# A graph layer on one core: two more quads of sender rows are loaded by ScalarE, and the last groups are taken in another order

## The chip, the core and the metric

The kernel runs on one core of a Trainium2 chip. The core has five engines that run side by side, each working through its own list of instructions in order: TensorE (PE, matrix products), VectorE (DVE), ScalarE (ACT), GpSimd (POOL) and SyncE (SP, which only issues transfers). They wait for each other through semaphores, which are counters. ScalarE, GpSimd and SyncE can issue transfers between the memory of the chip and that of the core. The metric is the device time of one execution in microseconds, lower is better.

## The reference, cut to what matters

There are 6250 nodes with 128 features each and 206,250 edges, sorted by receiver. Each edge gets a weight vector of 128 from two small networks over its 32 + 32 features. It is multiplied with the receiver's query and the sender's key and summed in 8 heads of 16, which gives one score for each head. The score scales the sender's value, and the results are summed for each receiver. The sum is added to the node's features, and a layer norm follows.

```python
w_ij = silu(edge_feats @ rad_W1 + rad_b1) @ rad_W2 + rad_b2
w_ij = w_ij + (silu(chi_scalar @ sph_W1 + sph_b1) @ sph_W2 + sph_b2)
q_i = (node_feats @ Wq)[receivers]; k_j = (node_feats @ Wk)[senders]; v_j = (node_feats @ Wv)[senders]
alpha = (q_i * w_ij * k_j).reshape(-1, 8, 16).sum(axis=-1) / sqrt(16) * cutoffs[:, None]
out = segment_sum(alpha[..., None] * v_j, receivers) / 16
x = layernorm(x + out)
```

All of it is in float32.

## The kernel before

Edges are worked on in **quads** of 512 (4 columns of 128) and **groups** of four quads (2048 edges). There are 403 quads in 101 groups; the last group has three. A group's quads are taken in the order 0, 2, 1, 3, and each place in this order is a **slot**. The loop in L583 to L643 goes over groups and slots. Inside a slot the calls are written out by hand, and this order is kept on every engine (`manual_schedule`, L191), so the order of the calls is the order in each engine's list.

First comes a stage over the nodes (L207 to L364). Keys and values of all nodes are put into one table in the chip's memory (`kv_tab`, 1 KB a node). Ten quads (`XQ`) get their keys and values there directly, from gathered node features.

In the loop, a quad goes through these steps:

- Its senders' rows of `kv_tab` have been fetched into the core. `gathers` (L144) does this with four indirect transfers issued by GpSimd (L121), each of 128 rows, into a ring of 16 buffers (`RING`), 14 slots ahead (`AHEAD`).
- For six quads (`ROW_QUADS`), spread evenly, `load_rows` (L152) does it instead through SyncE: for each of the 128 edges of a column one register load of four addresses (L164) and four transfers of 1 KB (L168), a few edges in each slot, done eight slots (`ROW_LEAD`) ahead of use. These have two buffers of their own.
- `q_and_hidden` (L416), in every even slot: queries of two quads at their edges (L414), and the first layer of the two quads that follow (L407), then its activation on ScalarE (L432).
- `weigh` (L435): second layer on TensorE (L439), bias on ScalarE, which makes `w` (L441). `multiply` (L446) makes `u` on VectorE, and `turn_back` (L452) transposes `u` in the next slot.
- `scores` (L458 to L461) multiplies with the keys and sums the heads; `messages` (L471) scales the values.
- `sum_quads` (L481) sums a group's messages for 32 receivers a quad. `part_sums` (L509), `place` (L503) and `sum_group` (L514, L516) put them at their rows and carry over what belongs to the next group.
- `statistics` (L520) makes the layer norm. It collects four groups (`LB`), except at the end, and `write_rows` (L543) sends one group a slot to the chip's memory through SyncE.

For group g + 2, `load_x` is issued in slot 0 of group g, and `load_feats` (L173) and `load_rel` (L182) in slot 1; all three go through SyncE. The features of group g + 2 are first used by TensorE in slot 2 of group g + 1. Every transfer that SyncE or ScalarE issues carries one of eight completion counters. The framework hands these round in the order in which it plans the transfers, and a transfer waits until the one before it on the same counter has landed.

The last group's sums go over 128 rows at once: `wide_one_hots` (L484) makes the matrices on VectorE, `sum_wide` (L495) the products. In the code before, the loop ends with the last quad turned but not yet scored. Then come the sums of the last group but one, the wide sums of two quads (L650 to L652), `statistics(g - 1)`, and the last quad in three pieces (L656), followed by its own layer norm (L660 to L672).

Behind all this stands a general version for inputs that break the sorted layout (L682 to L789). It is not run here.

Of the kernel before, what the change touches and what calls it, by code (L numbers as in the profile page):

```python
# [13 lines left out]
F32 = mybir.dt.float32  # L14
# [6 lines left out]
PSUM = bass.MemoryType.PSUM  # L21
DRAM = bass.MemoryType.DRAM
SP = mybir.EngineType.SP

P = 128
N = 6250
# [18 lines left out]
LB = 4  # L45
XQ = 10
RING = 16
ROW_QUADS = 6
ROW_LEAD = 8
CHECK = 20  # L50
NEIGHBORS = 16.0
# [5 lines left out]
def gnn_kernel(ctx, tc, x, src, dst, weight, edges, rad_W1, rad_b1, rad_W2, rad_b2,  # L57
# [24 lines left out]
    dst_i = const.tile([P, NT], I32, name="dst_i")  # L82
    src_i = const.tile([P, NT], I32, name="src_i")
    src_x = const.tile([P, math.ceil(XQ / NQ) * GT], I32, name="src_x")
    at_i = const.tile([P, ROW_QUADS * QT], I32, name="at_i")
    scale = const.tile([P, NT], F32, name="scale")
    w1 = const.tile([P, D], F32, name="w1")
    w2 = const.tile([P, 2, D], F32, name="w2")
# [16 lines left out]
    ends = const.tile([P, 8], F32, name="ends")  # L105
    general = const.tile([1, 1], I32, name="general")

    gp = ctx.enter_context(tc.tile_pool(name="group", bufs=2))
    ep = ctx.enter_context(tc.tile_pool(name="edge", bufs=2))


    aux = ctx.enter_context(tc.tile_pool(name="aux", bufs=1, space=PSUM))
# [4 lines left out]
    def quad_of(name, bufs, width=D):  # L117
        return ep.tile([P, QT, width], F32, name=name, bufs=bufs)
# [16 lines left out]
        else:  # L135
            pairs[-1].append(q)

    every = (len(order) - ROW_LEAD) // ROW_QUADS
    row_at = [(n + 1) * every for n in range(ROW_QUADS)]
    row_quads = {order[i] for i in row_at}  # L140
    feats_of, relb_of, act_of, kv_of, hot_of, hotT_of, x_of, q_of, msg_of = ({} for _ in range(9))
    po_of, part_of, to_of, tot_of, xT_of, y0_of, u_of, pick_of, pq_of = ({} for _ in range(9))

# [7 lines left out]

    def load_rows(i):  # L152

        k = max(i + ROW_LEAD - 1, 0) // every
        if k >= ROW_QUADS:
            return
        q, start = order[row_at[k]], max(k * every - ROW_LEAD + 1, 0)
        slots = row_at[k] - ROW_LEAD + 1 - start
        a, b = ((j * P + slots - 1) // slots for j in (i - start, i - start + 1))
        if i == start:  # L160
            kv_of[q] = quad_of("rows", 2, 2 * D)
        table = kv_tab.bitcast(U8).rearrange("(o n) b -> o (n b)", o=1)
        for p in range(a, min(b, P)):
            _, rows = nc.values_load_multi_w_load_instructions(  # L164
                at_i[p:p + 1, k * QT:(k + 1) * QT], engines=(SP,), min_val=0,
                max_val=(N - 1) * ROW_BYTES, skip_runtime_bounds_check_because="senders are nodes")
            for t in range(QT):
                nc.sync.dma_start(kv_of[q][p:p + 1, t, :].bitcast(U8),  # L168
                                  table[:, ds(rows[t], ROW_BYTES)])

    def load_feats(g):
        feats_of[g] = gp.tile([P, EG // 2], F32, name="feats")
# [34 lines left out]
    with tc.tile_pool(name="nodes", bufs=1) as nodes, \  # L207
# [145 lines left out]
                nc.sync.dma_start(scale, weight)  # L353
        for q in order[XQ:AHEAD]:
            gathers(q)
        for k, i in enumerate(row_at):
# [10 lines left out]
    with tc.tile_pool(name="ps", bufs=1, space=PSUM) as pp:  # L367
# [131 lines left out]
        def place(g):  # L499

            to = to_of[g] = gp.tile([P, 2, P], F32, name="to")
            if g < NG - 1:
                nc.vector.tensor_scalar(to[:, 0, :], colp, rowq[:, g:g + 1], None, op0=OP.is_equal)  # L503
            nc.vector.tensor_scalar(to[:, 1, :], colp, rowp[:, g:g + 1], None, op0=OP.is_equal)  # L504
# [13 lines left out]
            nc.scalar.activation(tot_of[g], ph[:, :D], AF.Copy)  # L518

        def statistics(g):  # L520
            first = g // LB * LB if g < NG - 2 else g
            if g == first:
                y0_of[g] = (gp.tile([P, LB, D], F32, name="y0"), gp.tile([P, LB, 2], F32, name="mv"))
            y0, mv = y0_of[first]
            k = g - first + 1
            nc.vector.tensor_tensor(y0[:, k - 1, :], tot_of[g], x_of[g], op=OP.add)
            st = gp.tile([P, 6], F32, name="st")
            nc.vector.bn_stats(st, y0[:, k - 1, :])
            nc.vector.bn_aggr(mv[:, k - 1, :], st)
            if k == LB or g >= NG - 3:  # L530
                sd = gp.tile([P, LB], F32, name="sd")
                nc.scalar.activation(sd[:, :k], mv[:, :k, 1], AF.Sqrt, bias=eps)
                rs = gp.tile([P, LB], F32, name="rs")
                nc.vector.reciprocal(rs[:, :k], sd[:, :k])
                shift = gp.tile([P, LB], F32, name="shift")
                nc.vector.scalar_tensor_tensor(shift[:, :k], mv[:, :k, 0], -1.0, rs[:, :k],
                                               op0=OP.mult, op1=OP.mult)
                for i in range(k):
# [44 lines left out]
        for g in range(NG):  # L583
            last = g == NG - 1
            for slot, j in enumerate((0, 2, 1, 3)):
# [22 lines left out]
                if 1 <= g:  # L608
                    for t in ((), (0, 1), (2, 3))[slot] if last else ((), (0, 1), (2,), (3,))[slot]:
                        sum_quads(g - 1, t)  # L610
                if before is not None:
                    alpha = scores(before, pu)
                multiply(q, w)
# [8 lines left out]
                if slot == 1:  # L622
                    if g + 2 < NG:
                        load_feats(g + 2)
                        load_rel(g + 2)
                    if 1 <= g:
                        place(g - 1)
                    if last:
                        place(g)
                        n = nc.values_load(general, min_val=0, max_val=1)  # L630
                if last:
                    wide_one_hots(q)
                write_rows()
                load_rows(i)
                if slot == 2 and g + 1 < NG:
                    one_hots_T(g + 1)
                if slot == 2 and 2 <= g:
                    statistics(g - 2)
                if slot == 3:
                    if g + 1 < NG - 1:  # L640
                        one_hots(g + 1)
                    if CHECK <= g < CHECK + len(checks):
                        checks[g - CHECK]()  # L643
        g = NG - 1
        pu = turn_back(before)
        part_sums(g - 1)
        sum_group(g - 1)
        po_of[g] = pp.tile([P, D], F32, name="po")
        done = [q for q in order[-quads_in(g):] if q != before]
        for q in done:  # L650
            for t in range(QT):
                sum_wide(q, t, start=(q == done[0] and t == 0))  # L652
        nc.tensor.matmul(po_of[g], to_of[g][:, 1, :], tot_of[g - 1], start=False, stop=False)
        statistics(g - 1)
        write_rows(LB)
        for t in (slice(0, 2), slice(2, 3), slice(3, 4)):  # L656
            messages(before, scores(before, pu, t), t)
            for i in range(t.start, t.stop):
                sum_wide(before, i, stop=(i == QT - 1))
        y = gp.tile([P, LB, D], F32, name="y0")[:, 0, :]  # L660
        nc.vector.tensor_tensor(y, po_of[g], x_of[g], op=OP.add)
        st = gp.tile([P, 6], F32, name="st")
        nc.vector.bn_stats(st, y)
        mv = gp.tile([P, LB, 2], F32, name="mv")[:, 0, :]
        nc.vector.bn_aggr(mv, st)
        sd = gp.tile([P, LB], F32, name="sd")
        nc.scalar.activation(sd[:, :1], mv[:, 1:2], AF.Sqrt, bias=eps)
        rs = gp.tile([P, LB], F32, name="rs")
        nc.vector.reciprocal(rs[:, :1], sd[:, :1])
        nc.vector.tensor_scalar(y, y, mv[:, 0:1], rs[:, :1], op0=OP.subtract, op1=OP.mult)  # L670

        nc.sync.dma_start(out[N - P:, :], y)  # L672

    manual.close()


    before = const.tile([P, P], F32, name="before")
    nc.vector.tensor_scalar(before, col, row, None, op0=OP.is_lt)
    spare = const.tile([P, 1], F32, name="spare")
    nc.vector.tensor_scalar(spare, row, float(NB * P), None, op0=OP.add)  # L680
# [100 lines left out]
    with tc.If(n == 0, preferred_fallthrough_block=False) as held:  # L781
        pass
    with held.Else():
        nc.sync.dma_start(acc[:N, :], x)
# [47 lines left out]
```

## Time and profile before

| | |
|---|---|
| time, median of 3 runs | 2098.6 us (2095.31 to 2099.16) |
| profiled execution, its own time | 2934.18 us |
| its span, first to last instruction | 2932.0 us |
| mean granted TensorE clock in it | 0.807 |
| GpSimd gathers from `kv_tab` | 1548, 945 ns each |
| rows of `kv_tab` loaded through SyncE | 768 register loads, 3072 transfers |
| ScalarE busy | 986.0 us (34%) |
| VectorE busy | 1458.2 us (50%) |

The profiled execution is 835.6 us longer than the median of the timed runs, so the shares of its span are not those of a timed run. Durations of single instructions, and the spacing of instructions in stretches where nothing stalls, can be read from it. In a row of the order of time, the first number is the start in us from the span's start, the second the length in us, then engine, line, operation and tiles; in brackets stand the idle time before it and what ended it. In a row of the waits stand who waited and for whom, then us in total, how many times, and the longest. In a tile row the three numbers behind the count are the shortest, median and longest duration in ns.

### The profile page before, as it was taken

How to read it: one execution, taken by the hardware profiler on the slowest of the kernel's cores; microseconds unless marked ns; L12 is line 12 of the kernel's file. 1: busy time of each engine (PE TensorE's matmuls, PEld its weight loads, DVE VectorE, ACT ScalarE, POOL GpSimd, SP SyncE). 2: the span in 40 equal slices, each digit the busy share in tenths (PEclk: the TensorE clock that was granted, in tenths of full speed). 3: DMA queues.
4: the chain of work that ended last, by engine and by line, in shares of the span. 5: the costliest groups of instructions: out<-in, count | busy, mean ns of one | idle time of the engine just before them, and what ended most of it. 6: DMA issues, size and time to landing. Idle time of an engine off the chain costs nothing.

```text
span 2932.0 us, 37165 instructions
## 1 busy us (share of the span) xinstructions
PE 2134.5 (73%) x9966; PEld 1018.8 (35%) x9966; DVE 1458.2 (50%) x3001; ACT 986.0 (34%) x1825; POOL 1502.0 (51%) x1596
## 2 busy tenths in 40 slices
PE   4776777777777777777777777676767777777777
PEld 3433333333333333333333333333333333333334
DVE  2444544545545544545455454454445545545457
ACT  1232333333332333333333333333333333323334
POOL 5355555545555545555554555545555555555540
PEclk6777878878778878888787887878778878888888
DMA  4433333333333333333333333333333333333330
GB/s 159 131 98 102 106 105 111 109 94 109 99 109 111 100 99 106 103 111 106 98 109 91 109 107 102 113 89 104 107 97 115 98 104 107 101 106 105 102 92 19
DMA packets 146344, 303.61 MB, mean 104 GB/s; under 512 B 36710, under 2 KB 79568, under 8 KB 146128
## 3 DMA queue, kind: packets, MB, share of 16 engines
q0 software_dynamic: 75584, 205.62, 24.0%
q1 hardware_dynamic: 69056, 95.15, 10.3%
q8 instruction: 81, 1.33, 0.2%
q14 instruction: 135, 1.11, 0.1%
q10 hardware_dynamic: 1488, 0.40, 0.1%
HBM read 287.58 MB, written 13.46 MB: 103 GB/s over the span
## 4 chain that ended last, share of the span: by engine, by line
PE 33%; another core or an unknown queue 16%; DVE 11%; issue 9%; ACT 5%; POOL 4%; DMA 1%; SPq 0%; DVEq 0%; ACTq 0%; POOLq 0%
PE ph L439 14%; PE pq L414 7%; PE pq L452 5%; PE ph L407 5%; POOL kv L121 4%; DVE m L458 3%; ACT w L441 3%; DVE u L446 3%; DVE msg L471 2%; ACT act L432 1%; PE po L481 1%; DVE side L460 1%; DMA kv<-kv_tab,src_i 1%; DVE to L504 0%
## 5 line engine op out<-in xcount | busy, mean ns | idle before, releaser
L121 POOL DMA_INDIRECT kv<-kv_tab,src_i x1548 | 1463.1, 945 | 1327.6 <-DVE msg L471 787.0
L439 PE MATMUL ph<-act,w 128*128 128x512 f32 x1612 | 954.0, 724 | 11.0 <-issue 9.2
L441 ACT ACTIVATE w<-ph,bsum 128x512 f32<-128x512 f32 x403 | 276.7, 687 | 1303.4 <-remote 467.6
L407 PE MATMUL ph<-feats,w 32*128 32x512 f32 x1612 | 631.0, 756 | 25.7 <-ACT w L441 23.4
L414 PE MATMUL pq<-hotT,q 32*128 32x512 f32 x806 | 385.2, 746 | 322.5 <-DVE m L458 312.9
L458 DVE TENSOR_TENSOR m<-pq,kv 128x512 f32<-128x512 f32 x399 | 274.0, 687 | 689.6 <-remote 520.7
L452 PE MATMUL pq<-ident,u 128*128 128x128 f32 x1612 | 311.8, 325 | 365.9 <-DVE u L446 267.6
L432 ACT ACTIVATE act<-ph,b 128x512 f32<-128x512 f32 x806 | 502.5, 686 | 216.3 <-PE ph L407 186.1
L446 DVE TENSOR_TENSOR u<-pq,w 128x512 f32<-128x512 f32 x403 | 277.5, 689 | 577.0 <-ACT w L441 303.0
L439 PEld LDWEIGHTS ph<-act,w 128*128 128x128 f32 x1612 | 342.1, 235 | 282.4 <-issue 277.0
L452 PEld LDWEIGHTS pq<-ident,u 128*128 128x128 f32 x1612 | 202.7, 162 | 532.9 <-issue 318.3
L414 PEld LDWEIGHTS pq<-hotT,q 32*128 32x128 f32 x806 | 101.7, 216 | 567.7 <-DVE m L458 371.3
L460 DVE TENSOR_REDUCE side<-m 128x32 f32<-128x512 f32 x405 | 280.4, 692 | 13.8
L471 DVE TENSOR_TENSOR msg<-kv,side 128x512 f32<-128x512 f32 x399 | 269.0, 674 | 0.1
L407 PEld LDWEIGHTS ph<-feats,w 32*128 32x128 f32 x1612 | 212.5, 223 | 161.1 <-issue 72.8
L481 PE MATMUL po<-msg,hot 128*32 128x128 f32 x3200 | 169.9, 313 | 0.0
L481 PEld LDWEIGHTS po<-msg,hot 128*32 128x32 f32 x3200 | 74.2, 117 | 154.0 <-issue 134.1
L518 ACT ACTIVATE tot<-ph 128x128 f32<-128x128 f32 x100 | 27.5, 275 | 197.6 <-PE ph L407 112.9
L249 PE MATMUL pk<-wkv,xT 128*128 128x256 f32 x178 | 52.3, 438 | 53.0 <-DVE kv L250 50.0
L461 DVE TENSOR_TENSOR side<-side,scale 128x32 f32<-128x32 f32 x405 | 80.7, 199 | 13.8
L387 PEld LDWEIGHTS ph<-wq,xT 128*128 128x128 f32 (+1 forms) x202 | 47.5, 236 | 70.3 <-issue 67.1
L250 DVE COPY kv<-pk 128x512 f32<-128x512 f32 (+1 forms) x45 | 30.1, 682 | 83.8 <-remote 56.1
(101 smaller groups left out, 966.9 us busy)
## 6 DMA issues: line engine op xcount, KB each, us to landing
feats<-in_edges SPq DMA_DIRECT2D x101, 512.0 KB
rows<-kv_tab SPq DMA_DIRECT2D x3072, 1.0 KB
kv<-kv_tab,src_i POOLq DMA_INDIRECT x1548
relb<-rel_lin SPq DMA_DIRECT2D x101, 128.0 KB
x<-in_x SPq DMA_DIRECT2D x101, 64.0 KB
out<-y SPq DMA_DIRECT2D x101, 64.0 KB
kv_tab<-kv SPq DMA_DIRECT2D x12, 512.0 KB
act<-in_x SPq DMA_DIRECT2D x12, 256.0 KB
```

Source lines behind the costliest of these rows:

```text
L121: nc.gpsimd.indirect_dma_start(out=o, out_offset=None, in_=table, in_offset=bass.IndirectOffsetOnAxis(ap=index, axis=0))
L407: nc.tensor.matmul(act_of[q, i], w1[r0:r0 + R, :], feats_of[g][r0:r0 + R, c0:c0 + EQ], start=True, stop=True)
L414: nc.tensor.matmul(pq_of[q], q_of[g][b, :], hotT_of[g][b, :], start=True, stop=True)
L432: nc.scalar.activation(act, act_of[n, i], AF.Silu, bias=b1[:, i:i + 1])
L439: nc.tensor.matmul(pw, w2[:, i, :], act_of[q, i], start=(i == 0), stop=(i == 1))
L441: nc.scalar.activation(w, pw, AF.Identity, bias=bsum)
L446: nc.vector.tensor_tensor(u_of[q], pq_of[q], w, op=OP.mult)
L452: nc.tensor.transpose(pu[:, t, :], u_of[q][:, t * P:(t + 1) * P], ident)
L458: nc.vector.tensor_tensor(m, pu[:, t, :], kv_of[q][:, t, :D], op=OP.mult)
L460: nc.vector.tensor_reduce(alpha, m.rearrange("p t (h e) -> p t h e", e=HD), AX.X, OP.add)
L471: nc.vector.tensor_tensor(msg_of[q][:, t, :].rearrange("p t (h e) -> p t h e", e=HD), kv_of[q][:, t, D:].rearrange("p t (h e) -> p t h e", ...
L481: nc.tensor.matmul(po_of[g][j * W:(j + 1) * W, :], hot_of[g][:, j * QT + t, :], msg_of[g * NQ + j][:, t, :], start=(t == 0), stop=(t == QT ...
```

## The change

Three things are changed.

1. **Two more quads** leave GpSimd's gathers. Their rows are loaded by ScalarE's queue in the same manner as SyncE's: a register load and four transfers for each of 128 edges. The quads stand at places 185 and 370 of the order. Their rows are issued in odd slots only (1 to 177 and 187 to 361), one or two edges a slot, at the end of the slot. They share one buffer of their own. SyncE's six quads stay as they are.
2. **The last two groups** are ordered anew. `place(g - 1)`, the wide one-hots and `statistics(g - 2)` of the last group come one or two slots earlier (one set of one-hots already in the last slot of the group before). The wide sums of its first quad are made in slot 2. The statistics go by shorter runs from the third last group on.
3. **The last quad** is taken in halves instead of pieces of 2, 1 and 1 columns. The layer norm of the last group but one is made between the halves, on two columns of shared tiles, and its write goes out just ahead of the last one.

Besides, two small VectorE instructions that only the general version needs move into that version, and the buffers of the loop are given back before it.

```diff
-ROW_QUADS = 6
+SP_QUADS, ACT_QUADS = 6, 2
...
+    loads = []
+    for engine, queue, n, end in ((SP, nc.sync, SP_QUADS, len(order) - ROW_LEAD),
+                                  (ACT, nc.scalar, ACT_QUADS, len(order) - 4 * ROW_LEAD)):
+        at = [(k + 1) * (end // n) for k in range(n)]
+        for k, i in enumerate(at):
+            begin = at[k - 1] + (1 - ROW_LEAD if engine == SP else 2) if k else 0
+            slots = range(begin, i - ROW_LEAD + 1)
+            loads.append((engine, queue, i, [j for j in slots if engine == SP or j % 2]))
+    row_quads = {order[i] for _, _, i, _ in loads}
...
+        for k, (engine, queue, at, slots) in enumerate(loads):
+            if i not in slots:
+                continue
+            q, n = order[at], len(slots)
+            a, b = ((j * P + n - 1) // n for j in (slots.index(i), slots.index(i) + 1))
+            if i == slots[0]:
+                kv_of[q] = quad_of(*("rows", 2) if engine == SP else ("rows_act", 1), 2 * D)
+            for p in range(a, min(b, P)):
+                _, rows = nc.values_load_multi_w_load_instructions(
+                    at_i[p:p + 1, k * QT:(k + 1) * QT], engines=(engine,), min_val=0,
...
+                for t in range(QT):
+                    queue.dma_start(kv_of[q][p:p + 1, t, :].bitcast(U8),
+                                    table[:, ds(rows[t], ROW_BYTES)])
...
-            first = g // LB * LB if g < NG - 2 else g
+            first = g // LB * LB if g < NG - 3 else g
...
-            if k == LB or g >= NG - 3:
+            if k == LB or g >= NG - 4:
...
+                if last and slot == 2:
+                    po_of[g] = pp.tile([P, EQ], F32, name="ph", bufs=4)[:, :D]
+                    for t in range(QT):
+                        sum_wide(order[i - 2], t, start=(t == 0))
...
-                    if 1 <= g:
+                    if 1 <= g < NG - 1:
                         place(g - 1)
                     if last:
+                        wide_one_hots(g * NQ + 1)
                         place(g)
+                        statistics(g - 2)
...
-                if last:
-                    wide_one_hots(q)
+                if last and slot == 0:
+                    wide_one_hots(g * NQ + 2)
+                    place(g - 1)
                 write_rows()
                 load_rows(i)
...
-                if slot == 2 and 2 <= g:
+                if slot == 2 and 2 <= g < NG - 1:
                     statistics(g - 2)
                 if slot == 3:
...
+                    if g + 1 == NG - 1:
+                        wide_one_hots((g + 1) * NQ)
...
-        statistics(g - 1)
+        halves = (slice(0, QT // 2), slice(QT // 2, QT))
+        messages(before, scores(before, pu, halves[0]), halves[0])
+        for t in range(QT // 2):
+            sum_wide(before, t)
+        moments(0, tot_of[g - 1])
+        alpha = scores(before, pu, halves[1])
+        nc.vector.reciprocal(rs[:, 0:1], sd[:, 0:1])
+        nc.vector.scalar_tensor_tensor(shift[:, 0:1], mv[:, 0, 0:1], -1.0, rs[:, 0:1],
+                                       op0=OP.mult, op1=OP.mult)
+        messages(before, alpha, halves[1])
+        for t in range(QT // 2, QT):
+            sum_wide(before, t, stop=(t == QT - 1))
+        nc.scalar.activation(ys[:, 0, :], ys[:, 0, :], AF.Identity, scale=rs[:, 0:1],
+                             bias=shift[:, 0:1])
+        written.append((g - 1, ys[:, 0, :]))
         write_rows(LB)
-        for t in (slice(0, 2), slice(2, 3), slice(3, 4)):
-            messages(before, scores(before, pu, t), t)
-            for i in range(t.start, t.stop):
-                sum_wide(before, i, stop=(i == QT - 1))
...
+        moments(1, po_of[g])
```

`moments(k, total)` adds the node features to a total, takes its mean and variance on VectorE and the root on ScalarE.

More of the change, by code (lines that the diff above doesn't have):

```diff
@@ L23 @@
 SP = mybir.EngineType.SP
+ACT = mybir.EngineType.Activation
 P = 128
@@ L84, in gnn_kernel @@
     src_x = const.tile([P, math.ceil(XQ / NQ) * GT], I32, name="src_x")
-    at_i = const.tile([P, ROW_QUADS * QT], I32, name="at_i")
+    at_i = const.tile([P, (SP_QUADS + ACT_QUADS) * QT], I32, name="at_i")
     scale = const.tile([P, NT], F32, name="scale")
@@ L106, in gnn_kernel @@
     general = const.tile([1, 1], I32, name="general")
-    gp = ctx.enter_context(tc.tile_pool(name="group", bufs=2))
-    ep = ctx.enter_context(tc.tile_pool(name="edge", bufs=2))
+    pools = ctx.enter_context(ExitStack())
+    gp = pools.enter_context(tc.tile_pool(name="group", bufs=2))
+    ep = pools.enter_context(tc.tile_pool(name="edge", bufs=2))
     aux = ctx.enter_context(tc.tile_pool(name="aux", bufs=1, space=PSUM))
@@ L136, in gnn_kernel @@
             pairs[-1].append(q)
-    every = (len(order) - ROW_LEAD) // ROW_QUADS
-    row_at = [(n + 1) * every for n in range(ROW_QUADS)]
-    row_quads = {order[i] for i in row_at}
+    loads = []
[7 more added lines that the diff above has]
+    row_quads = {order[i] for _, _, i, _ in loads}
     feats_of, relb_of, act_of, kv_of, hot_of, hotT_of, x_of, q_of, msg_of = ({} for _ in range(9))
@@ L152, in load_rows @@
     def load_rows(i):
[L154 to L161, printed above, removed]
-        table = kv_tab.bitcast(U8).rearrange("(o n) b -> o (n b)", o=1)
[L163 to L169, printed above, removed]
+        table = kv_tab.bitcast(U8).rearrange("(o n) b -> o (n b)", o=1)
+        for k, (engine, queue, at, slots) in enumerate(loads):
[8 more added lines that the diff above has]
+                    at_i[p:p + 1, k * QT:(k + 1) * QT], engines=(engine,), min_val=0,
+                    max_val=(N - 1) * ROW_BYTES,
+                    skip_runtime_bounds_check_because="senders are nodes")
+                for t in range(QT):
+                    queue.dma_start(kv_of[q][p:p + 1, t, :].bitcast(U8),
+                                    table[:, ds(rows[t], ROW_BYTES)])
     def load_feats(g):
@@ L355, in gnn_kernel @@
             gathers(q)
-        for k, i in enumerate(row_at):
+        for k, (_, _, i, _) in enumerate(loads):
             nc.vector.tensor_scalar(at_i[:, k * QT:(k + 1) * QT],
@@ L647, in gnn_kernel @@
         sum_group(g - 1)
[L648 to L652, printed above, removed]
-        nc.tensor.matmul(po_of[g], to_of[g][:, 1, :], tot_of[g - 1], start=False, stop=False)
-        statistics(g - 1)
-        write_rows(LB)
-        for t in (slice(0, 2), slice(2, 3), slice(3, 4)):
-            messages(before, scores(before, pu, t), t)
-            for i in range(t.start, t.stop):
-                sum_wide(before, i, stop=(i == QT - 1))
@@ L660, in gnn_kernel @@
[L660 to L669, printed above, removed]
@@ L670, in gnn_kernel, with moments @@
-        nc.vector.tensor_scalar(y, y, mv[:, 0:1], rs[:, :1], op0=OP.subtract, op1=OP.mult)
+        for t in range(QT):
+            sum_wide(order[-2], t)
+        nc.tensor.matmul(po_of[g], to_of[g][:, 1, :], tot_of[g - 1], start=False, stop=False)
+        ys, mv, sd, rs, shift = (gp.tile([P, LB, D], F32, name="y0"), gp.tile([P, LB, 2], F32, name="mv"),
+                                 *(gp.tile([P, LB], F32, name=o) for o in ("sd", "rs", "shift")))
+        def moments(k, total):
+            nc.vector.tensor_tensor(ys[:, k, :], total, x_of[g - 1 + k], op=OP.add)
+            st = gp.tile([P, 6], F32, name="st")
+            nc.vector.bn_stats(st, ys[:, k, :])
+            nc.vector.bn_aggr(mv[:, k, :], st)
+            nc.scalar.activation(sd[:, k:k + 1], mv[:, k, 1:2], AF.Sqrt, bias=eps)
@@ new lines, in gnn_kernel @@
+        for t in range(QT // 2, QT):
[3 more added lines that the diff above has]
+        written.append((g - 1, ys[:, 0, :]))
+        write_rows(LB)
+        moments(1, po_of[g])
+        nc.vector.reciprocal(rs[:, 1:2], sd[:, 1:2])
+        y = ys[:, 1, :]
+        nc.vector.tensor_scalar(y, y, mv[:, 1, 0:1], rs[:, 1:2], op0=OP.subtract, op1=OP.mult)
@@ L672, in gnn_kernel @@
         nc.sync.dma_start(out[N - P:, :], y)
     manual.close()
[L677 to L680, printed above, removed]
+    pools.close()
     def scatter_add(index, values):
@@ L783, in gnn_kernel @@
     with held.Else():
+        before = const.tile([P, P], F32, name="before")
+        nc.vector.tensor_scalar(before, col, row, None, op0=OP.is_lt)
+        spare = const.tile([P, 1], F32, name="spare")
+        nc.vector.tensor_scalar(spare, row, float(NB * P), None, op0=OP.add)
         nc.sync.dma_start(acc[:N, :], x)
```

## The prediction

> **What bounds the kernel now.** I read the page first, then the waits, then the order of time of single engines.
>
> The page's busy row, clock row and costliest group:
>
> ```profile
> PE 2134.5 (73%) x9966; PEld 1018.8 (35%) x9966; DVE 1458.2 (50%) x3001; ACT 986.0 (34%) x1825; POOL 1502.0 (51%) x1596
> ...
> PEclk6777878878778878888787887878778878888888
> ...
> L121 POOL DMA_INDIRECT kv<-kv_tab,src_i x1548 | 1463.1, 945 | 1327.6 <-DVE msg L471 787.0
> ```
>
> The waits:
>
> ```profile
> POOL kv L121 <- DVE msg L471: 787.0, 191, 24.4
> DVE m L458 <- remote: 534.0, 90, 8.8
> ACT w L441 <- remote: 467.6, 108, 10.3
> ```
>
> In this execution POOL waits for ring buffers, so TensorE's side looks like the bound. But it took 2934.2 us (span 2932.0, 2.2 around it), 836 more than the median 2098.6. The chain holds 16% "unknown" and 9% "issue", 733 us of waits with no cause in the kernel; they come about once a group, and the clock halves after them. The timed runs have no room for them, so I build them from undisturbed stretches. POOL in order of time (start, length, idle before):
>
> ```profile
> 142.90 0.94 POOL L121 DMA_INDIRECT kv<-kv_tab,src_i  x1 [24.37 <-DVE msg L471]
> 144.15 0.95 POOL L121 DMA_INDIRECT kv<-kv_tab,src_i  x1 [0.30 <-issue]
> ```
>
> Back to back, a gather comes every 1.25 us. Of 1548 gathers 24 are done before the ring first fills; the others run from 142.9: 1524 x 1.25 = 1905, to 2048. The last lands 2.4 later (packets of isolated gathers).
>
> TensorE, undisturbed, at full clock (weighing matmuls of five slots):
>
> ```profile
> 2885.61 1.88 PE L439 MATMUL ph<-act,w 128*128 128x512 f32 x4
> ...
> 2889.89 1.88 PE L439 MATMUL ph<-act,w 128*128 128x512 f32 x4
> ...
> 2893.84 1.88 PE L439 MATMUL ph<-act,w 128*128 128x512 f32 x4
> ...
> 2898.42 1.88 PE L439 MATMUL ph<-act,w 128*128 128x512 f32 x4
> ...
> 2902.38 1.88 PE L439 MATMUL ph<-act,w 128*128 128x512 f32 x4
> ```
>
> Four slots take 16.77 us; POOL needs 4 x 4 x 1.25 x 64/65 = 19.7. SyncE's rows (tile view; then one row's four transfers):
>
> ```profile
> L164 SPq TENSOR_LOAD <-at_i x768: 2/558/1378, 131.5 to 2804.0; - x192
> ```
>
> ```profile
> 1498.15 1.27 SPq L168 DMA_DIRECT2D rows<-kv_tab  x4
> ```
>
> A row is 0.61 to the first register move, 0.07, 1.27: 1.95 us, also the lower quartile from row to row. 768 rows are 1498; feats, relb, x and out of a group are 0.46 + 0.65 + 1.2 + 1.2, 101 times 3.5: 354. Less 17 for the last five groups, SP's work from 131.5 ends at 1966 with slot 382. TensorE may be four slots ahead of SP, so 16 to 20 slots of 4.19 and the end (20) follow: 2053 to 2070.
>
> The end, from the score of the last quad but one:
>
> ```profile
> 2912.34 0.68 DVE L458 TENSOR_TENSOR m<-pq,kv 128x512 f32<-128x512 f32 x1
> ...
> 2920.80 0.29 DVE L526 TENSOR_TENSOR y<-tot,x 128x128 f32<-128x128 f32 x1 [3.08 <-ACT tot L518]
> ...
> 2922.31 0.42 DVE L458 TENSOR_TENSOR m<-pq,kv 128x256 f32<-128x256 f32 x1
> ...
> 2928.02 0.34 DVE L670 TENSOR_SCALAR y<-y,mv,rs 128x128 f32<-128x128 f32 x1
> ```
>
> m of quad 401 to the span's end is 19.7. Its rows land 5.0 before the last ones, so POOL's sum is 2049.1 - 5.0 + 19.7 + 2.2 = 2066; SP's end is equal within its error; TensorE alone would be near 1850. The median is 32 (1.5%) above: two servers of nearly equal pace, each waiting for the other at times, or a gather of 1.27. I take POOL as the bound, with SP just behind.
>
> **The change part by part.**
>
> *POOL.* Two quads less: 8 x 1.25 = 10.0 us (10.2 at 1.27; nothing where something else binds, rival 2). The two DVE conversions more (0.16 each) before the first group are below notice.
>
> *ScalarE.* 256 rows: one register load and four transfers each. ScalarE's other register load took 0.47, its small transfers 0.33 to 0.45 against SP's 0.23 to 0.37; at SP's price 1.95 a row, at ScalarE's own up to 2.3: 500 to 590 us on an engine with 986 us of activations. They stand in odd slots, 1 or 2 rows, behind tot and xT (or q), ahead of part and the next w. Between two w's lie 4 to 5 us, of which two rows take 3.9 to 4.6 from 0.75 on: w is late by 0 to 0.6 in a slot of two rows, 44% of odd slots. Who waits for w is u on DVE, then TensorE's turn; u has 0.4 of reserve (2905.43 against w's end at 2904.99). Price: below 0.2 a group.
>
> The Trainium skill ("DMA: Bandwidth & Descriptors", "Issuing engines are not separate DMA queues") says that issuing from more engines saves only sequencer time, usually small beside the transfer. The row says the opposite weight: 1.95 us of sequencer against a 0.05 us packet. By the rule SP could take these rows too at little cost; by the row that is 499 us on top of 1852, beyond the kernel's time. I take the row: ScalarE is the only place, and POOL's 10 us stand.
>
> *A tie that the diff doesn't show.* All transfers of SP and ScalarE share eight completion counters, handed round in a planned order, and each waits for the eighth before it. In the planned order ScalarE runs 4 to 5 slots ahead of SP: its rows wait for SP's of 5 or 6 slots earlier (harmless), but SP's rows of slot s now wait for ScalarE's of s + 4. SP's order holds the feats of group g too: in about 60 of 88 groups they now go out only after ScalarE's first row of slot 4g - 3, one slot before TensorE needs them; before they could be five slots early. Priced from that slot's weighing start: xT at 2.67 (2892.56 against 2889.89), + 0.68 to the issue, + 0.95 to landing = 4.3; feats land 3.3 after: 7.6. TensorE asks at 5.76 (2895.65). At its own pace it waits 1.9 (16.77 becomes 18.6); at POOL's, 0.9. Both stay below 19.7, and the ring of 16 quads levels the rest. SP's own 18.8 (7.9 rows x 1.95 + 3.5) becomes 19.0 to 19.6 where it must wait for ScalarE's next rows: still below 19.7, by little. In the first 58 slots SP has 2.2 rows a slot (20.7 a group), above POOL: there waits of 0.3 over 14 groups land on the path. I take 2 of these 4 us; the ends are 0 and, with SP as the bound, 60 x 0.8 = 48.
>
> The skill's rule that speaks against it ("TensorE: Matmul & The Clock Gate", "Why this matters for your kernels"): a TensorE gap over about 3 us brings the half clock back. The trace agrees: after a 7.0 us gap the four matmuls took
>
> ```profile
> 1522.26 3.62 PE L439 MATMUL ph<-act,w 128*128 128x512 f32 x4
> ```
>
> instead of 1.88. By the row's waits (0.9 to 1.9) the gate stays open and costs nothing; by the rule, were feats 1.5 later still, each of 60 groups would pay up to 1.7 more, about 100 us. I take nothing.
>
> *The end.* Before, m of the last quad starts 7.0 after the message before it is done (2915.2): one-hots, the statistics of g - 2 and, behind ScalarE's three y's, tot, then g - 1. Those move to earlier slots or between the halves. New: four wide sums now stand ahead of the turn on TensorE (0.8 to 1.5), so m starts near 2916.0; half one 1.45, moments 0.8, half two 1.05, reciprocal and shift 0.35, message 0.4: 2920.1; sum 0.7, moments 0.85, root 0.3, reciprocal 0.2, scale 0.35: 2922.5 against 2928.4, 5.9 less. The statistics now in slot 1 add 1.6 to DVE there, of which 1.1 shows: -4.8. The last rows (5.0 after the others) still arrive in time. On SP the write of group g - 1 now stands close ahead of the last one: its y is ready at 2920.6, its issue takes 1.2, so it is gone by 2921.9 and hidden; were it 1 us later, it would show in full from 2922.5 on.
>
> **Sum:** -10.0 - 4.8 + 2.0 = -12.8 on 2098.6: 2086. The percentage by which timed runs exceed my sum is left as it is.
>
> **Rivals.** (1) *The tie sets the pace, slower.* Place: feats in slot 4g - 3. SP has no reserve if its 1.95 us holds, and no longer a five-slot lead to smooth uneven groups. With 0.25 us a chained group (60 x 0.25 = 15) the gain is gone; 0.4 to 0.9 gives 2107 to 2138. For it: SP's sum equals POOL's. Against: SP waited 199.5 us for TensorE before feats, so it is not always late. (2) *SP was the bound already:* POOL's 10 are hidden, the end alone is gained: 2092 to 2097. (3) *The end gains nothing,* since its DVE work only moved: 2088 to 2091.
>
> **How the numbers follow.** 0.2% (4.2 us) is about what this kernel's runs can tell. Full or nearly full gain, with (3): 0.48, at 2078 to 2092. (2): 0.18, half of it faster by over 0.2%. (1): 0.34, two thirds of it below 2120. So faster 0.56, same 0.11, slower 0.33. The likeliest case's own range is 2078 to 2092; 2074 to 2120 leaves out about 0.15.
>
> **What would show it.** Right: 1540 gathers at 1.25; ScalarE's rows near 2 us; TensorE's wait before the hidden matmuls of slot 2 below 2; under 15 us from the last quad but one to the end. Wrong: SP waiting on ScalarE's rows for a large total, TensorE's hidden matmuls waiting 3 us and more for feats in most groups, or ScalarE rows of 3 us.

## The result, and the profile after

The changed kernel takes 2379.11 us (median; 2364.19 to 2390.36), the kernel before 2096.95 beside it: a ratio of 1.136 (95% interval 1.133 to 1.139), 282 us slower. The prediction was 2086, with 2074 to 2120 as its range. The profiled execution took 2382.61 (span 2380.8), so unlike that of before it stands for the timed runs.

The lines of the page that answer to those of before, and TensorE's two costliest groups:

```profile
PE 1990.5 (84%) x9966; PEld 959.7 (40%) x9966; DVE 1463.6 (61%) x2999; ACT 968.9 (41%) x1828; POOL 1496.7 (63%) x1588
...
PEclk9998888888898998888898898988888989888999
...
L123 POOL DMA_INDIRECT kv<-kv_tab,src_i x1540 | 1456.8, 946 | 786.0 <-issue 386.4
L448 PE MATMUL ph<-act,w 128*128 128x512 f32 x1612 | 871.9, 669 | 5.2 <-ACT act L441 5.1
L416 PE MATMUL ph<-feats,w 32*128 32x512 f32 x1612 | 530.0, 721 | 171.4 <-DMA feats<-in_edges 152.5
```

The gathers last as long as before. Of GpSimd's 786 us of idle time 386 are the 0.3 us that lie between any two gathers, and 320 are waits for ring buffers to come free: it is not what the kernel waits for. The waits of the engines (who waited for whom; us in total, times, longest):

```profile
POOL kv L123 <- DVE msg L480: 319.8, 93, 10.3
...
ACT w L450 <- DMA rows_act<-kv_tab: 164.5, 38, 6.6
...
ACT part L518 <- DMA rows_act<-kv_tab: 156.2, 54, 4.3
PE ph L416 <- DMA feats<-in_edges: 152.5, 65, 4.3
...
DVE hotT L402 <- DMA relb<-rel_lin: 149.8, 64, 4.6
```

ScalarE's two lines are mostly the time that it takes to issue its rows, for which the activations behind them stand still. TensorE waits for `feats` and VectorE for `relb`; both come from SyncE. So the question is what holds SyncE. Its own waits:

```profile
SPq L177 <- DMA rows_act<-kv_tab: 167.0, 96, 5.3
SPq L182 <- DMA rows_act<-kv_tab: 62.9, 43, 5.6
...
SPq L177 <- DMA feats<-in_edges: 38.8, 29, 2.6
SPq L197 <- DMA rows_act<-kv_tab: 22.3, 12, 3.9
...
SPq L556 <- DMA rows_act<-kv_tab: 13.7, 7, 3.3
...
SPq L191 <- DMA rows_act<-kv_tab: 7.7, 17, 0.9
```

In front of its own rows (L177), features (L182), receiver rows (L191), node rows (L197) and writes (L556), SyncE waits for ScalarE's rows, for data that none of them uses: 167.0 + 62.9 + 22.3 + 13.7 + 7.7 = **273.6 us**, nearly the whole loss. This is the tie through the shared completion counters. The counters that the trace names for the 4546 transfers of the two engines fit one round of eight. In it, where a transfer of SyncE's rows stands behind one of ScalarE's rows, that is in 587 of 625 cases one of three or four slots later.

One group in order of time (start, length; SyncE, ScalarE, TensorE and VectorE together, other lines left out). It shows what SyncE's wait does next:

```profile
730.08 1.88 PE L448 MATMUL ph<-act,w 128*128 128x512 f32 x4
...
733.29 1.57 ACTq L177 DMA_DIRECT2D rows_act<-kv_tab  x4
...
734.02 1.88 PE L448 MATMUL ph<-act,w 128*128 128x512 f32 x4
...
735.27 0.37 SPq L182 DMA_DIRECT2D feats<-in_edges  x1
735.82 0.55 SPq L191 DMA_DIRECT2D relb<-rel_lin  x1
...
739.02 0.66 PE L416 MATMUL ph<-feats,w 32*128 32x512 f32 x1 [2.07 <-DMA feats<-in_edges]
...
740.16 2.42 ACT L441 ACTIVATE act<-ph,b 128x512 f32<-128x512 f32 x4 [3.53 <-PE ph L416]
740.84 0.69 DVE L402 TENSOR_TENSOR hotT<-relb,side 128x512 f32<-128x512 bf16 x1 [2.49 <-DMA relb<-rel_lin]
...
742.84 1.06 PE L448 MATMUL ph<-act,w 128*128 128x512 f32 x1
```

The `feats` go out 0.4 us after ScalarE's row is issued. TensorE can start the hidden layer 3.75 us after that, having stood idle for 2.07. The activations follow until 742.58, and only then comes the next weighing: 8.8 us after the one before, where groups with early `feats` take 4.8 (14 groups with a single row in slot 4g - 3). The `relb` behind the `feats` are later still, and VectorE stops 2.49 us for them. Sorted by the planned order of the counters, groups 6 to 89 fall into two kinds (with two left over): in 58 the `feats` stand behind ScalarE's row of slot 4g - 3, in 24 behind a row two slots earlier. From the weighing of slot 4g - 3 to that of slot 4g + 1, the four slots in which these `feats` are asked for, the first kind takes 25.0 us on average and the second 19.5.

### The profile page after: what moved, and what is told of

The parts are those of the page before. It is cut to its first block, busy times and chain, and to the rows that moved or that the text cites. A ratio compares the mean times of both kernels' runs of the same rounds, so it can differ in the third digit from the quotient of the medians.

```text
span 2380.8 us, 39420 instructions
## 1 busy us (share of the span) xinstructions
PE 1990.5 (84%) x9966; PEld 959.7 (40%) x9966; DVE 1463.6 (61%) x2999; ACT 968.9 (41%) x1828; POOL 1496.7 (63%) x1588
## 3 DMA queue, kind: packets, MB, share of 16 engines
q14 instruction: 153, 1.25, 0.2%
## 4 chain that ended last, share of the span: by engine, by line
PE 44%; DMA 20%; ACT 10%; issue 7%; DVE 6%; SPq 6%; ACTq 3%; POOL 3%; DVEq 0%; POOLq 0%
PE ph L448 20%; PE ph L416 11%; DMA feats<-in_edges 10%; PE pq L461 7%; DMA rows_act<-kv_tab 6%; ACT w L450 5%; PE pq L423 4%; SPq L177 3%; DVE u L455 3%; ACT act L441 2%; ACTq L177 2%; POOL kv L123 2%; PE po L490 2%; DMA x<-in_x 2%; POOL msg L123 2%
## 5 line engine op out<-in xcount | busy, mean ns | idle before, releaser
L448 PE MATMUL ph<-act,w 128*128 128x512 f32 x1612 | 871.9, 669 | 5.2 <-ACT act L441 5.1
L416 PE MATMUL ph<-feats,w 32*128 32x512 f32 x1612 | 530.0, 721 | 171.4 <-DMA feats<-in_edges 152.5
L441 ACT ACTIVATE act<-ph,b 128x512 f32<-128x512 f32 x806 | 488.6, 689 | 276.2 <-PE ph L416 275.9
L461 PE MATMUL pq<-ident,u 128*128 128x128 f32 x1612 | 294.0, 311 | 150.4 <-DVE u L455 150.0
L448 PEld LDWEIGHTS ph<-act,w 128*128 128x128 f32 x1612 | 315.4, 218 | 246.0 <-issue 234.0
L423 PE MATMUL pq<-hotT,q 32*128 32x512 f32 x806 | 341.5, 693 | 2.2 <-DVE m L467 2.2
L416 PEld LDWEIGHTS ph<-feats,w 32*128 32x128 f32 x1612 | 184.5, 209 | 366.2 <-issue 279.8
L402 DVE TENSOR_TENSOR hotT<-relb,side 128x512 f32<-128x512 bf16 x101 | 69.2, 685 | 149.8 <-DMA relb<-rel_lin 149.8
L518 ACT ACTIVATE part<-po 128x128 f32<-128x128 f32 x100 | 27.6, 276 | 215.2 <-DMA rows_act<-kv_tab 156.2
L388 PE MATMUL ph<-pick,x 128*128 128x128 f32 (+1 forms) x202 | 42.7, 294 | 42.9 <-DMA x<-in_x 36.6
```

Source lines behind the costliest of these rows:

```text
L416: nc.tensor.matmul(act_of[q, i], w1[r0:r0 + R, :], feats_of[g][r0:r0 + R, c0:c0 + EQ], start=True, stop=True)
L423: nc.tensor.matmul(pq_of[q], q_of[g][b, :], hotT_of[g][b, :], start=True, stop=True)
L441: nc.scalar.activation(act, act_of[n, i], AF.Silu, bias=b1[:, i:i + 1])
L448: nc.tensor.matmul(pw, w2[:, i, :], act_of[q, i], start=(i == 0), stop=(i == 1))
L461: nc.tensor.transpose(pu[:, t, :], u_of[q][:, t * P:(t + 1) * P], ident)
```

## The experiments

Two theories stood at the start. *Late features*: the lag of SyncE behind ScalarE in the plan makes features late in 58 groups, wherever SyncE's load stands. *ScalarE's rows*: bursts of two rows on ScalarE make `w` late. A third came out of the first runs: *SyncE's list is full*. It set the pace already, so every wait put into it lengthens the kernel by its own length. All times below are medians; "list" is the span of the profiled execution less all waits of SyncE.

| kernel: quads on SyncE + ScalarE | time, us | SyncE waits, us | of these on ScalarE's rows | list, us |
|---|---|---|---|---|
| 6 + 0, new end | 2093.65 | 232.4 | - | 1860.0 |
| 6 + 2 odd slots (the change) | 2379.11 | 510.3 | 273.6 | 1870.5 |
| 6 + 2 every slot | 2239.02 | 365.7 | 123.5 | 1871.2 |
| 8 + 0 | 2594.92 | 206.9 | - | 2387.1 |
| 5 + 0 | 2014.75 | 411.6 | - | 1600.9 |
| 5 + 2 odd slots | 2096.95 | 483.3 | 210.7 | 1606.6 |
| 5 + 2 every slot | 2008.85 | 402.3 | 27.1 | 1604.9 |
| 4 + 2 odd slots | 2047.93 | 688.7 | 77.1 | 1357.0 |
| 4 + 2 every slot | 2017.96 | 664.4 | 3.2 | 1350.1 |

The kernels before that ran beside them had medians of 2090.61 to 2096.95.

**The end alone, 6 + 0.**

```diff
-SP_QUADS, ACT_QUADS = 6, 2
+SP_QUADS, ACT_QUADS = 6, 0
```

With none on ScalarE the division that spreads the quads is by `max(n, 1)` besides.

> The changed kernel with no quad on ScalarE: SyncE's six quads and the new order of the last two groups stay. Theory of the tie (SyncE runs four slots behind ScalarE because of the shared counters, so features and receiver rows come late): no ScalarE rows, no tie, so the loop is that of the kernel before, with 1548 gathers; only the end differs, by my sum -4.8: 2092 (2088 to 2096). Rival, the new end is itself to blame for part of the loss: above 2110. Rival, the end gains nothing: 2095 to 2099.

2093.65 against 2090.61, a ratio of 1.0012 (1.0000 to 1.0025). The end is not what made the change slower, and it wins nothing here. This profile is the first of the old loop that is not stretched. Waits of its engines, VectorE's and TensorE's on SyncE's transfers and GpSimd's on the ring:

```profile
DVE hotT L402 <- DMA relb<-rel_lin: 84.5, 49, 4.6
...
PE ph L416 <- DMA feats<-in_edges: 66.7, 42, 4.6
...
POOL kv L123 <- DVE msg L480: 21.9, 35, 3.9
```

and SyncE's:

```profile
SPq L177 <- DMA relb<-rel_lin: 54.5, 75, 1.6
...
SPq L182 <- PE ph L416: 14.5, 6, 6.7
```

TensorE waits for `feats` without any tie, while SyncE waits for TensorE's hidden matmuls, before it may load the next features, only 14.5 us: SyncE is behind from its own work. Of its 232.4 us of waits 49 lie ahead of its first row and 77 behind its last one. Between the two (70.4 to 1999.1) lie 106, and 54.5 of them are for the landing of its own receiver rows, again on a shared counter. So a list with waits in it can still be full.

**Four quads on SyncE, two on ScalarE.**

```diff
-SP_QUADS, ACT_QUADS = 6, 2
+SP_QUADS, ACT_QUADS = 4, 2
```

> The same 256 ScalarE rows in the same slots, but SyncE with four quads instead of six. SyncE's planned work then no longer lags: its features wait for a ScalarE row two slots before their own place instead of four slots behind it. 1548 gathers, as in the kernel before. Tie theory: groups fall from 23.3 us to about GpSimd's 19.7, so 2090 to 2110. Rival, ScalarE's own rows set the pace (bursts of two rows take 4.05 us and w is late): the rows are unchanged, so 2330 to 2400.

2047.93, a ratio of 0.980 (0.978 to 0.983) to before: faster than the tie theory allowed, with the same 1548 gathers as before. So GpSimd didn't set the pace of the kernel before either. ScalarE's rows are the same, in the same slots, and the kernel is 331 us shorter than the change: they are not the cause by themselves. GpSimd is not the bound here either: its last gather starts at 1988.6, and the span ends 57 us later.

**Features and receiver rows on ScalarE's queue.**

```diff
-        nc.sync.dma_start(feats_of[g], edges[g])
+        (nc.scalar if g > 1 else nc.sync).dma_start(feats_of[g], edges[g])
...
-        nc.sync.dma_start(relb_of[g], r[:, None, :].to_broadcast([NQ, W, EQ]))
+        (nc.scalar if g > 1 else nc.sync).dma_start(relb_of[g], r[:, None, :].to_broadcast([NQ, W, EQ]))
```

> The changed kernel (6 quads on SyncE, 2 on ScalarE, the plan still four slots apart for the rows), but the features and the receiver rows of a group are issued by ScalarE's queue in their old slot, five slots before use. They are then not behind SyncE's tied rows. Tie theory, by way of late features and receiver rows: the 58 long groups (25.0 us) fall to the length of the others (19.4 us), so 2380 - 58 x 5.6 = 2055, held up by GpSimd's 19.7: 2080 to 2110. Rival, SyncE's list itself is full (18.8 a group plus 3.1 of waits): it loses only 1.1 a group, 2380 - 98 = 2280. Rival, ScalarE's rows set the pace: 2390 to 2430, since ScalarE gets 0.6 more a group.

2478.83: slower still, and all three expectations miss. TensorE no longer waits for `feats`, and the kernel gets 100 us longer. SyncE's waits first, then ScalarE's:

```profile
SPq L177 <- DMA rows_act<-kv_tab: 351.1, 166, 8.9
SPq L177 <- DMA rows<-kv_tab: 113.6, 141, 2.3
SPq L177 <- DMA feats<-in_edges: 63.0, 23, 6.1
```

```profile
ACT w L450 <- DMA rows_act<-kv_tab: 380.7, 54, 8.8
...
ACT w L450 <- DMA relb<-rel_lin: 136.2, 24, 6.1
```

SyncE's list is shorter by 103 us (1767.8), but its waits on ScalarE's rows grew to 372.5, and ScalarE, whose transfers stand in the same ring of counters, was itself held before `w`. So features that come in time do not help by themselves. But this edit also put more transfers of ScalarE ahead of SyncE's rows, so the run alone does not refute *late features*; the change with a row in every slot, below, speaks against it.

**Four and four, odd slots.** The edit is the one line, with 4, 4.

> Four quads on SyncE and four on ScalarE: as many quads taken from GpSimd as in the changed kernel, twice the rows on ScalarE (512, three in many odd slots), and in the plan the two queues side by side (features wait for a ScalarE row two slots before their own place). Tie theory: no long groups from late features, GpSimd as in the change, 2075 to 2110, plus what w is late in slots of three rows: to 2150. Rival, ScalarE's rows set the pace: twice the loss of the change, 2600 to 2700.

2726.27: far above the tie theory. ScalarE becomes the bound. The chain that ended last, by engine:

```profile
PE 37%; ACTq 29%; ACT 13%; issue 9%; DMA 5%; DVE 4%; SPq 1%; POOL 1%; DVEq 0%; POOLq 0%
```

Three rows in a slot take 6.0 us on ScalarE from the first transfer to the end of the last, more than an undisturbed slot of 4.2. That the loss lies above what I gave for ScalarE's rows (2600 to 2700) doesn't revive it for the change, whose odd slots hold one or two rows.

**Five quads on SyncE, none on ScalarE**, and **eight and none.** The edit is that of the end alone, with 5, 0 and 8, 0.

> The changed kernel without rows on ScalarE and with five quads on SyncE instead of six: 1552 gathers, 4 more than before. If SyncE set the pace of the kernel before (its list less its waits is 1860.0 us of a span of 2092.4 with six quads), 128 rows x 1.95 = 250 us less on it hands the pace to GpSimd, which with 1548 gathers gave 2048: 2052 (2045 to 2060). If GpSimd set the pace, as the prediction took it: +5 to 2096 to 2100.

> All eight quads of rows on SyncE, none on ScalarE: 1540 gathers as in the changed kernel, no tie. SyncE full already: 256 rows x 1.95 = 499 more, 2093 + 499 = 2593 (2560 to 2610), above the changed kernel's 2379. Rival, SyncE still had room for some of it and the loss in the change comes from ScalarE alone: 2100 to 2350.

2014.75, and 2594.92 against a forecast of 2593. From six to eight quads a row costs (2594.92 - 2093.65) / 256 = 1.96 us of the kernel's time: the list is full at six. From six to five the kernel gains 79 us although GpSimd has four gathers more; then something else sets the pace. With five, GpSimd's gathers come every 1.251 us from 53.8 to 1994.1, with a single longer step of 1.81, and SyncE waits for others (SyncE's waits):

```profile
SPq L556 <- ACT y L548: 128.5, 23, 22.5
SPq L182 <- PE ph L416: 99.7, 42, 6.2
```

So GpSimd's pace is 2015 (2010 for the 1548 gathers of before, at 1.25 us each), and SyncE's was 2092. The 5 + 0 forecast of 2052 was 37 too high because it took GpSimd's pace from the 4 + 2 run, where GpSimd was done 57 us before the end, against 18 here.

**Five and two, odd slots, then every slot.** The second has, besides 5, 2:

```diff
-            loads.append((engine, queue, i, [j for j in slots if engine == SP or j % 2]))
+            loads.append((engine, queue, i, list(slots)))
```

> Five quads on SyncE, two on ScalarE in odd slots as in the change: SyncE stays three to four slots behind ScalarE in the plan (its rows wait for ScalarE rows of 3 or 4 slots later), but its list is 250 us shorter. If the loss of the change is SyncE's waits on ScalarE's rows, added to a full list: the 274 us of waits come, at the same size, on 1842 (1860 - 250 + 232 of other waits), 2116 at most, and part of the room is used up by waits that now replace others: 2045 to 2116, likeliest 2070. If the lag alone makes the loss, however full SyncE is (features chained to a late row in 60 groups and more): 2200 to 2350. If ScalarE's bursts of two rows do it: 2330 to 2400; that is already unlikely, since four quads and two gave 2048.

> As the run with five and two quads, but ScalarE's rows in every slot, so at most one a slot: no bursts of two, and in the plan no lag (SyncE's rows wait for ScalarE rows one slot earlier). 1544 gathers. Both theories of the tie: GpSimd's pace, 2043 (2035 to 2060). If it is no faster than the run before it, neither lag nor bursts matter with five quads.

2096.95 (ratio 1.0025, 1.0008 to 1.0041) and 2008.85; the second was forecast 34 higher, from the same pace of GpSimd. With room in SyncE's list (odd slots), 210.7 us of waits on ScalarE's rows, and the bursts, cost only 82 us against 5 + 0. The other waits fell from 411.6 to 272.6, so 139 us of the tie took the place of waiting that was there anyway. It is no clean test of the lag, though: its rows stand behind ScalarE's of three or four slots later as in the change, but the features of only 10 groups, not of 60, stand behind the row of slot 4g - 3. In every slot, with neither bursts nor lag, the tie shrinks to 27.1 us and the kernel is the fastest of all: a ratio of 0.959 (0.957 to 0.962) to before.

**The kernel before with five quads.**

```diff
-ROW_QUADS = 6
+ROW_QUADS = 5
```

> The kernel before, old end and all, with five quads of rows instead of six; beside the run with five and none (the new end, 2014.75) it prices the new end under GpSimd's pace. My step: the new end is worth 4.8, so 2019.5 (2017 to 2022). Rival, it is worth nothing here too, as with six quads (2093.65 against 2090.61): 2012 to 2016. Both say that one quad less on SyncE is worth about 75 us.

2015.34 (2014.18 to 2017.21) against 2014.75 (2014.35 to 2016.9) with the new end: the end is worth nothing that these runs can tell.

**The change with ScalarE's rows in every slot, 6 + 2.**

> The changed kernel with ScalarE's rows in every slot, one at most: no bursts of two, but SyncE full with six quads and in the plan still three to four slots behind ScalarE. Theory (full list + waits on ScalarE's rows): the waits come in smaller steps but remain, 2094 + 100 to 200: 2190 to 2290, and the trace's waits of SyncE on ScalarE's rows, added to 2094, give the time within 20. Rival, the bursts of two rows made the loss of the change: below 2110. Rival, the lag costs a fixed 5.6 us in each of some 60 groups: 2340 to 2400.

2239.02. SyncE's waits on ScalarE's rows, the two largest of them:

```profile
SPq L177 <- DMA rows_act<-kv_tab: 96.1, 83, 4.1
...
SPq L182 <- DMA rows_act<-kv_tab: 17.9, 18, 2.5
```

All of them make 123.5. 2094 + 123.5 is 2217, 22 below the time and so just outside the 20 that I had allowed; 11 of these are the longer list (1871.2). The bursts alone would have left it below 2110. A fixed loss per chained group would have put it above 2340, and 60 groups still have their features behind ScalarE's row of slot 4g - 3 or the slot before. Neither holds.

**Five and three, every slot.**

> Five quads on SyncE, three on ScalarE in every slot (one row, sometimes two): 1540 gathers as in the changed kernel. GpSimd's pace, from the run with five and none: 2014.75 - 12 x 1.25 = 1999.7; the run with five and two was 4 above its own such sum, so 2004 (1998 to 2020). If three quads are too many for ScalarE (as four in odd slots were): above 2060.

2180.88: a third quad is too much for ScalarE even one row at a time. Waits of this kernel, against 190.3 and 108.6 with five and two:

```profile
DVE u L455 <- ACT w L450: 338.0, 229, 6.4
...
ACT w L450 <- DMA rows_act<-kv_tab: 295.3, 81, 7.3
```

Here SyncE isn't full (its list is 1605.6). Where a transfer of ScalarE's rows stands behind one of SyncE's rows, that is now in 609 of 813 cases one of the same slot, against 258 of 744 with five and two. Whether that or the 128 rows more make `w` late isn't told apart.

**Four and two, every slot.**

> Four quads on SyncE and two on ScalarE in every slot. Against the run with four and two in odd slots (2047.9) it prices the bursts of two rows alone, since neither has a lag in the plan. Gathers 1548: GpSimd's pace is 2014.75 - 4 x 1.25 = 2009.8; with the 4 us that the run with five and two stood above its sum, 2014 (2008 to 2020), so bursts cost 34 in 70 pairs. Rival, ScalarE's 256 rows cost what they cost wherever they stand: 2040 to 2055.

2017.96 against 2047.93 in odd slots, as forecast: the bursts of two rows cost up to 30 us, 0.34 a group. The tie's waits fell too, from 77.1 to 3.2, in a list that has over 600 us of other waits; how much of the 30 us is theirs isn't told apart.

**What follows.** With six quads on SyncE its list stays at 1860 to 1871 us and its waits other than on ScalarE's rows at 232 to 242, tie or none. So the spans of the three runs differ by the tie: 2092.4, + 123.5 + 11.2 + 9.8 = 2236.9, and + 273.6 + 10.5 + 4.3 = 2380.8. That the tie's waits stay where there is no room for them and vanish partly where there is (five quads) is what the full list foretells. Two things stay open. The 10.5 us by which the list got longer have no cause here. And a kernel in which the two engines have counters of their own wasn't tried, so the counters are named by the instructions' waits, not by taking them away.

## Why the prediction was wrong

*What bounds the kernel: wrong, and the first cause.* The prediction took GpSimd at 2066 as the bound with SyncE "just behind" at 2053 to 2070. The runs show GpSimd at 2015 and SyncE at 2092. Two terms failed. (a) The start: 142.9 for GpSimd's 25th gather and 131.5 for SyncE's first row were read from a stretched execution. Undisturbed, that gather is at 84.4 (5 + 0) and that row at 70.4 (6 + 0), so the sums began 58 and 61 us too late. (b) SyncE's waits: the sum had none. From its first row to the end of its last one it had 1835 us; the 6 + 0 run takes 1928.7. The price of a row was not the fault: the mean from row to row, where no other transfer lies between, is 2.10, but 2.00 without waits. What is missing are the 106 us of waits between rows, half of them behind SyncE's own receiver rows. A start too late and waits left out partly cancelled for SyncE; GpSimd was left with the first alone. So the 1.5% by which the median lay above the sum was SyncE, not "two servers of nearly equal pace".

*GpSimd, -10.0: right in size, but off the path.* The 1540 gathers of 946 ns are 1.25 us apart, with 320 us of waits for buffers. Rival (2), SyncE already the bound, held for the kernel before; it had 0.18, and its forecast of 2092 to 2097 left the tie out.

*ScalarE: the cost of a row right, its price too low.* A single row takes 1.47 us for its four transfers and 0.49 for the register load (priced 1.95 to 2.3 together), two rows 4.05 with the second one's register load. Their price was given as below 0.2 a group and came to at most 0.34. The rule of the Trainium skill weighed there ("DMA: Bandwidth & Descriptors", "Issuing engines are not separate DMA queues") would have let SyncE take the rows at little cost. The 8 + 0 run measures 501 us for it, where the row's working gave 499. Here the measurement decides against the rule's "usually small": with rows of 1 KB the issue, 1.96 us a row, is what the kernel pays for.

*The tie: the mechanism and place right, the size wrong by a factor of more than 100.* 2.0 us were taken, with 48 as the upper end; it is 274. The step that failed is "Both stay below 19.7, and the ring of 16 quads levels the rest". It compared the tie with GpSimd's pace, when SyncE had no reserve at all. With SyncE as the bound each of its waits counts in full, in all the 90 or so groups that have rows on ScalarE (273.6 / 90 = 3.0 a group). The prediction let waits land on the path only in the first 14 groups, at 0.3 each; it was so everywhere. The offsets in slot 4g - 3 were too early as well. From the weighing start, over the 34 chained groups with one row there: ScalarE's first transfer at 4.03 (priced 3.35), `feats` out at 5.86 (4.3), TensorE's hidden matmuls at 9.98 (7.6). The weighing behind them came at 14.56, against 8.79 in the 14 groups of one row whose `feats` stand behind an earlier row: 5.8 later where I had 1.9. `relb` was not in the sum at all; VectorE started `hotT` at 11.77 instead of 8.24, and how much of the 5.8 that adds isn't told apart.

*Rival (1), the tie sets the pace:* this is what happened, but its 2107 to 2138 came from 0.4 to 0.9 us in 60 groups, the same undersized term.

*The clock gate, "I take nothing":* there was a cost, of open size. The same matmuls were busy 1990.5 us against 1808.7 in the 6 + 0 run, at a granted clock of 0.884 against 0.928. TensorE's waits for `feats` averaged 2.3 us (152.5 over 65) instead of 0.9 to 1.9, and 13 of them were over 3 us, the length that the rule names ("TensorE: Matmul & The Clock Gate", "Why this matters for your kernels"), against 4 in the 6 + 0 run. The rule alone does not place the half clock here: of 55 slots whose four weighing matmuls took over 3 us instead of 1.88, 35 had no gap of 3 us in the 8 us before. How much of the 182 us lies on the path can't be told.

*The end, -4.8: the working right, the gain not.* From `m` of the last quad but one to the end:

```profile
2365.89 0.69 DVE L467 TENSOR_TENSOR m<-pq,kv 128x512 f32<-128x512 f32 x1 [0.69 <-PE pq L423]
...
2374.97 0.35 DVE L699 TENSOR_SCALAR y<-y,mv,rs 128x128 f32<-128x128 f32 x1
```

it is 14.9 us (2380.8 - 2365.89) instead of 19.7. But with five quads that same `m` starts 2.7 us later with the new end (first row) than with the old one:

```profile
1997.27 0.69 DVE L467 TENSOR_TENSOR m<-pq,kv 128x512 f32<-128x512 f32 x1 [0.69 <-PE pq L423]
```

```profile
1994.58 0.68 DVE L458 TENSOR_TENSOR m<-pq,kv 128x512 f32<-128x512 f32 x1
```

The one-hots and statistics now lie ahead of it, for which I had charged 1.1. The profiles differ by 2.3, the timed medians by 0.6: rival (3).

## What to carry to other kernels

Before an engine is handed work that waits on another, find out which queue has no room, from an undisturbed execution: sum its list with the waits that stay in it, and check by taking one unit of work away (five quads instead of six: 79 us) before adding any. Two queues that share completion counters wait for each other's transfers without sharing data. A wait put into a full list costs its whole length, while in a list with room part of it replaces waiting that was there. When the same work is dealt to a second queue, small even pieces (one row in every slot) cost far less than pairs in every other slot: 2239 instead of 2379, and 2009 instead of 2097, where the lag in the plan went as well.

## What was not expected of the hardware

A burst of two rows on ScalarE took 4.05 us on average from the first transfer to the end of the last, against 1.47 for one, so the second cost 2.6, above the 1.95 to 2.3 that were priced. `feats` landed 4.0 us after their issue in the groups where TensorE waited for them, and 3.9 in the 6 + 0 run, where 3.3 had been taken. `relb`, a quarter of their size, took longer, 5.3 us in both runs; why isn't shown.
